# The softmax shift subtracted from adj^T square by square, into a second DRAM array

## Chip, cores and metric

One core of one Trainium2 chip runs the whole program. The metric is the device time of one execution in microseconds (us); the median of three runs of the kernel before is 11289.27 us (11283.2 to 11291.34).

## What is computed

Four graph layers over 3327 nodes with 128 features. All but the last 821 us of the execution go to the first, an attention layer with 128 heads (`d` below) of 8 elements each, whose scores are 3327 x 3327 in every head:

```python
q = (x @ Wq.T).reshape(d, n, h)
k = (x @ Wk.T).reshape(d, n, h)
v = (x @ Wv.T).reshape(d, n, h)
a = jnp.einsum('dnh,dmh->dnm', q, k) * scale
a = a + spatial_encoding + edge_encoding      # both are adj: a + 2 adj
a = jax.nn.softmax(a, axis=2)
out = jnp.einsum('dnm,dmh->dnh', a, v)
out = out.reshape(n, h * d)
return out @ Wo.T
```

The three later layers each multiply adj (or its transpose) with a 3327 x 128 array; layers 1, 2 and 3 read adj^T from DRAM, unshifted. The softmax needs a number per row n that is subtracted from the scores before the exponential. The kernel takes an upper bound: the largest adj in the row plus a bound of the row's products. It doesn't depend on the head, so it can be subtracted from adj itself.

## The kernel before

**Stages.** The first 451 us project x to q, k and v and write them to DRAM. The main stage (451 to 10332 us) is the attention. Then come the output projection (10332 to 10470 us) and the other layers, which stream adj^T and adj as "strips".

**Main stage.** The transposed scores are computed: partitions hold m, the free axis holds n. The columns n are cut into 7 blocks `c` of 476 (the last of 472). Within a block, 32 groups `g` of 4 heads follow each other, and within a group 13 pairs `q` of row tiles of 128 (26 tiles cover m). There are 7 x 32 x 13 = 2912 pairs. For each pair:

- VectorE *seeds* two PSUM banks with the adj^T tile minus the shift (`seed`, L640, tile `a` of 128 x 476, one for each of the 26 row tiles of the block);
- TensorE adds the products of the four heads one after the other (`scores`, L646), each time after ScalarE has taken the exponential of what is there (`exps`, L658 for two banks at once, L661 for one);
- TensorE multiplies the exponentials with the values (`values`, L699); VectorE copies the group's sums out (L707) and GpSimd's queue stores them (L711).

In the pairs q = 0, 4 and 8 one of the exponentials is made on VectorE instead (`hand_exp`): nine instructions L672, L674, L676, L678, four of L681, L683, spread over the pairs q, q+1, q+2 and q+3, in that order two, three, three and one.

**Order.** The stage is written out in program order by hand (`tc.manual_schedule`). Each engine and each queue works through its instructions in that order; nothing in the queues of SP (which issues most DMAs) and GpSimd is tied to the pair in which it is written, other than by what it waits for. `loads` issues the next group's keys, queries and values on SP (`load_qk`, 40 DMAs L553 to L557, and `load_v`, L570, in the pair q = 1), and GpSimd work on them (`negate_q` L565, `spread_v` L575, `all_here` L579) in the pair q = 4. The first scores of the next group wait for L579.

**Block ends.** In the last group of a block (g = 31) `load_shift` loads the next block's 476 shifts, broadcast to all partitions, and `load_adj` brings its 26 tiles `a` from `adjT` (L585), after each of which GpSimd subtracts the shift (L586). The pool of these tiles has 28 buffers: 26 in use, 2 ahead.

**Background squares.** adj^T is made during the main stage, one block ahead: 128 rows of adj at a time (a *square* `s`; 26 in all, the first four in the first stage, 22 in the main stage, planned at the block's first pair by `plan_squares`, one every 7 groups, in the groups 7k+1 and following). `plan(u, f)` runs f in program order at the pair u. A square takes four groups to load its rows (L285), transpose them on VectorE into `cols` (128 x 26 x 128, L290) and take row maxima (L294). Then `store` writes `cols` to `adjT` (L297, one DMA of 1664 KB), `gather` writes the maxima to DRAM (L301, 4 DMAs), `back` reads them back in another layout (`four`, L306, on SP), `finish` reduces `four` on VectorE (L310, L311) and stores the bound to `bound_d` (L312, on SP). Here store and gather stand at the last pair of the fourth group (u-1), back at pair 5 of the next one (u+5) and finish at its pair 12 (u+12). `cols` has one buffer.

**After the main stage.** `xs`, a second copy of x to which the layer's output is added (L892), is loaded into the pool `const` (L804), which is open from the start. The program puts that load where its memory is free: its three DMAs stand among the first on SP's queue. After the main stage, SP's queue has biases and weights (L811 to L853), two loads of attention output (`ot`, L877) with a strip of adj^T (L993) after each, then `w_raw` and `wo` (L861, L867), which TensorE's first transposes there need.

Of the kernel before, what the change touches and what calls it, by code (L numbers as in the profile page):

```python
# [10 lines left out]
F32 = mybir.dt.float32  # L11
# [6 lines left out]
ALU = mybir.AluOpType  # L18
# [4 lines left out]
P = 128  # L23
# [4 lines left out]
NT = 26  # L28
NP = NT * P
NQ = NT // 2  # L30
# [6 lines left out]
CW = 476  # L37
# [30 lines left out]
def rows_of(t):  # L68
    return P - 1 if t == NT - 1 else P
# [6 lines left out]
def pieces(m):  # L76

    return [(0, 112), (112, m)] if m == P - 1 else [(0, m)]


def width_of(c):

    return min(CW, N + 1 - c * CW)


def squares_of(c):

    return 0 if c < 0 else -(-min(CW * (c + 1), NP) // P)
# [3 lines left out]
def gnn_kernel(ctx: ExitStack, tc: tile.TileContext, x, adj, Wq, Wk, Wv, Wo, embed, layer,  # L92
               embed_bias, layer_bias, weight, bias, W_in, W_out, out):
    nc = tc.nc
    dram = ctx.enter_context(tc.tile_pool(name="dram", bufs=1, space=DRAM))
    const = ctx.enter_context(tc.tile_pool(name="const", bufs=1))
# [3 lines left out]

    adjT = dram.tile([NP, NP], F32, name="adjT")
    by_tile = adjT.rearrange("(p t) n -> t p n", t=NT)
    v_d = dram.tile([NP, HD], F32, name="v_d")
    n2_d = {s: dram.tile([GP], F32, name=f"n2{s}_d") for s in "qk"}
    kraw_d = dram.tile([H, GP], F32, name="kraw_d")
# [5 lines left out]
    bound_d = dram.tile([NP], F32, name="bound_d")  # L111
# [154 lines left out]
    class Square:  # L266
# [26 lines left out]
        def largest(self, j):  # L293
            nc.vector.tensor_reduce(self.rm[:, j:j + 1], self.rows, axis=AX.X, op=ALU.max)  # L294

        def store(self):
            nc.sync.dma_start(by_tile[:, :, self.s * P:(self.s + 1) * P].rearrange("t p n -> p t n"), self.cols)  # L297

        def gather(self):
            for i in range(4):  # L300
# [27 lines left out]
    with tc.tile_pool(name="a1", bufs=1) as a1, tc.tile_pool(name="a2", bufs=2) as a2, \  # L328
# [3 lines left out]
        xs = load_x(a1)  # L332
# [19 lines left out]
        for t0 in range(0, NT, 2):  # L352
            for s in "kq":
# [88 lines left out]
    with tc.tile_pool(name="d1", bufs=1) as d1, tc.tile_pool(name="d2", bufs=2) as d2, \  # L442
# [17 lines left out]
        with tc.If(loose > 0):  # L460
            for s in range(squares_of(0), NT):
                square(d2, s, d2)
            for t in range(NT):
                m = rows_of(t)
# [4 lines left out]
                with tc.For_i(0, HEADS, 1) as d:  # L469
# [3 lines left out]
                    for r in range(2):  # L473
                        for b in range(4):
# [9 lines left out]
                                                    op=ALU.max)  # L484
# [4 lines left out]
            for c in range(NC):  # L489
                c0 = c * CW  # L490
                w = min(CW, N - c0)
# [3 lines left out]
                with tc.For_i(0, HEADS, 1) as d:  # L495
# [12 lines left out]
                    for t in range(NT):  # L508
                        m = rows_of(t)
                        s = d_ps.tile([P, 4 * P], F32, name="ps_y")  # L510
# [13 lines left out]

    with tc.tile_pool(name="e1", bufs=1) as e1, tc.tile_pool(name="e_adj", bufs=28) as e_adj, \
            tc.tile_pool(name="e2", bufs=2) as e2, tc.tile_pool(name="e_e", bufs=1) as e_e, \
            tc.tile_pool(name="e_t", bufs=1) as e_t, tc.tile_pool(name="e_h", bufs=1) as e_h, \
            tc.tile_pool(name="e_ps", bufs=1, space=PSUM) as e_ps:  # L530
# [37 lines left out]
        def load_v(c, g):  # L568
            v = e2.tile([P, 4, NT * H], F32, name="VR", bufs=1)
            nc.sync.dma_start(v, bass.AP(tensor=v_d.tensor, offset=v_d.offset + 4 * g * N * H,  # L570
                                         ap=[[NT * H, P], [N * H, 4], [1, NT * H]]))
            return v

        def spread_v(c, g, v):
            nc.gpsimd.tensor_copy(VA[(c * NG + g) % 2][:, :, :, 0:H], v.rearrange("p j (t e) -> p t j e", e=H))  # L575

        def all_here(c, g):

            return nc.gpsimd.tensor_copy(seen, KT[(c * NG + g) % 2][:, :, 0].bitcast(F32))  # L579

        def load_adj(c, t, shift):

            a = e_adj.tile([P, CW], F32, name="a")
            w = width_of(c)
            nc.sync.dma_start(a[:, :w], by_tile[t, :, c * CW:c * CW + w])  # L585
            nc.gpsimd.tensor_tensor(a[:, :w], a[:, :w], shift[:, :w], op=ALU.subtract)  # L586
            return a

        def load_shift(c):
            s = e2.tile([P, CW], F32, name="shb", bufs=1)  # L590
            nc.sync.dma_start(s[:, :width_of(c)], bound_d[c * CW:c * CW + width_of(c)].unsqueeze(0)
                              .to_broadcast([P, width_of(c)]))
            return s

        with tc.If(loose < 1), tc.manual_schedule():
# [11 lines left out]
            n = len(pairs)  # L607
            adj_of, shift_of, v_of, e_of, here = {}, {}, {}, {}, {}
# [104 lines left out]
            def loads(u):  # L713

                c, g, q = pairs[u]
                k = c * NG + g
                if k + 1 < NC * NG:
                    nxt = divmod(k + 1, NG)
                    if q == 1:
                        load_qk(*nxt)  # L720
                        v_of[k + 1] = load_v(*nxt)
                    if q == 4:
                        negate_q(*nxt)
                        spread_v(*nxt, v_of.pop(k + 1))
                        here[k + 1] = all_here(*nxt)
                if c + 1 < NC and (g, q) == (0, 0):
                    plan_squares(c)
                if g == NG - 1 and c + 1 < NC:
                    if q == 0:
                        shift_of[c + 1] = load_shift(c + 1)  # L730
                        adj_of[c + 1] = []
                    while len(adj_of[c + 1]) < min(NT, 2 * q + 4):
                        adj_of[c + 1].append(load_adj(c + 1, len(adj_of[c + 1]), shift_of[c + 1]))


# [2 lines left out]
            def plan(u, f, *a):  # L738
                behind.setdefault(u, []).append((f, a))

            def plan_squares(c):
                for k, s in enumerate(range(squares_of(c), squares_of(c + 1))):
                    sq, u = Square(e_t, s), (c * NG + 7 * k + 1) * NQ
                    for j in range(4):
                        plan(u, sq.load, j)
                        plan(u + 7, sq.turn, j, 0)
                        plan(u + 11, sq.turn, j, 1)
                        plan(u + 12, sq.largest, j)
                        u += NQ
                    plan(u - 1, sq.store)  # L750
                    plan(u - 1, sq.gather)
                    plan(u + 5, sq.back)
                    plan(u + 12, sq.finish)

            v0 = load_v(0, 0)
            load_qk(0, 0)
# [12 lines left out]
            for i in range(-4, 4 * n + 15):  # L769
                u, j = in_slot(i)  # L770
# [16 lines left out]
                u = (i - 14) // 4  # L787
# [4 lines left out]
                if at % 2:  # L792
                    for k in (1, 2):
                        u, j = in_slot(i + k)
                        if 0 <= u < n:
                            scores(u, j)
                    u, r = ((i - 11) // 4, 0) if at == 3 else ((i - 13) // 4, 1)
# [3 lines left out]
                    loads(i // 4)  # L801


    xs = load_x(const)  # L804
    wts = ctx.enter_context(tc.tile_pool(name="wts", bufs=1))
    ones = wts.tile([P, 1], F32, name="ones")
    nc.vector.memset(ones, 1.0)

# [49 lines left out]
    with tc.tile_pool(name="f1", bufs=1) as f1, tc.tile_pool(name="f2", bufs=4) as f2, \  # L858
# [16 lines left out]
        for t0 in range(0, NT, 2):  # L875
# [5 lines left out]
                                    op=ALU.mult)  # L881
# [153 lines left out]
    with tc.tile_pool(name="g1", bufs=1) as g1:  # L1035
# [6 lines left out]
        a, aa = arr("a", D + 1), sm.new()  # L1042
# [12 lines left out]
        f = sm.div(sm.artanh(yn, L1_MAX_TANH), yn)  # L1055
# [33 lines left out]
    with tc.tile_pool(name="h1", bufs=1) as h1:  # L1089
# [4 lines left out]
        a, aa = arr("a", D + 1), sm.new()  # L1094
# [9 lines left out]
        f = sm.mul(sm.div(sm.artanh(pn, L2_MAX_TANH), pn), pf)  # L1104
# [8 lines left out]
        u, rr = arr("y"), sm.new()  # L1113
# [9 lines left out]
        t1 = sm.ts(sm.act(un, AF.Tanh), L2_MIN_NORM, ALU.max)  # L1123
# [10 lines left out]
    with tc.tile_pool(name="i1", bufs=1) as i1:  # L1134
# [67 lines left out]
```

## Time and profile before

| what | us |
|---|---|
| median of three runs | 11289.27 |
| the profiled execution | 11292.81 |
| its span, first to last instruction | 11290.9 |
| first stage | 451 |
| main stage, 451 to 10332 | 9881 |
| output projection, 10332 to 10470 | 138 |
| other layers | 821 |
| ScalarE busy in the main stage | 9810.12 |
| VectorE busy in the main stage | 7717.34 |
| GpSimd busy in the main stage | 1820.45 |

Times are those of one profiled execution, in microseconds unless marked ns. PE is TensorE, PEld its weight loads, DVE VectorE, ACT ScalarE, POOL GpSimd, SP the engine that issues most DMAs; SPq is the issue of a DMA. A group is listed by line, engine, operation and `out<-in` by the program's tile names. PEclk is the clock that TensorE was granted, as a share of full speed. In a timeline the columns are start, duration, engine, line, operation, and in square brackets the idle time before and what ended it.

### The profile page before, as it was taken

How to read it: one execution, taken by the hardware profiler on the slowest of the kernel's cores; microseconds unless marked ns; L12 is line 12 of the kernel's file. 1: busy time of each engine (PE TensorE's matmuls, PEld its weight loads, DVE VectorE, ACT ScalarE, POOL GpSimd, SP SyncE). 2: the span in 40 equal slices, each digit the busy share in tenths (PEclk: the TensorE clock that was granted, in tenths of full speed). 3: DMA queues.
4: the chain of work that ended last, by engine and by line, in shares of the span. 5: the costliest groups of instructions: out<-in, count | busy, mean ns of one | idle time of the engine just before them, and what ended most of it. 6: DMA issues, size and time to landing. Idle time of an engine off the chain costs nothing.

```text
span 11290.9 us, 205366 instructions
## 1 busy us (share of the span) xinstructions
PE 10774.9 (95%) x72980; PEld 3655.0 (32%) x72980; DVE 8367.4 (74%) x13563; ACT 10113.3 (90%) x13718; POOL 2021.8 (18%) x3261
## 2 busy tenths in 40 slices
PE   4599999999999999999999999999999999998779
PEld 2133333333333333333333333333333333334444
DVE  5577777778777787777777777777777777777633
ACT  3599999999999999999999999999999999996210
POOL 5211112111121111211112111121111211111000
PEclk8799999999999999999999999999999999999889
DMA  8755555555555554555555555555554544444447
GB/s 252 247 94 93 97 89 107 94 93 97 89 106 95 92 96 77 107 94 92 97 89 108 93 93 97 89 107 94 93 94 78 105 83 82 83 82 116 157 181 272
DMA packets 652681, 1243.36 MB, mean 110 GB/s; under 512 B 185966, under 2 KB 527990, under 8 KB 635148
## 3 DMA queue, kind: packets, MB, share of 16 engines
q1 hardware_dynamic: 609768, 1100.61, 50.0%
q0 software_dynamic: 41888, 129.51, 3.8%
q8 instruction: 591, 9.68, 0.4%
q14 instruction: 434, 3.56, 0.1%
HBM read 1082.90 MB, written 146.60 MB: 109 GB/s over the span
## 4 chain that ended last, share of the span: by engine, by line
ACT 72%; issue 12%; PE 9%; DVE 3%; DMA 1%; POOL 0%; SPq 0%; DVEq 0%; POOLq 0%; ACTq 0%
ACT e L658 60%; ACT e L661 11%; PE pu L995 5%; PE po L699 2%; PE S L646 1%; DVE e L681 1%; DVE S L640 0%; PE pu L947 0%; DMA ot<-oT_d 0%; DVE xs L982 0%; PE pu L970 0%; PE ps_y L891 0%; PE pu L958 0%; DVE h L676 0%; DMA QS<-qS_d 0%
## 5 line engine op out<-in xcount | busy, mean ns | idle before, releaser
L658 ACT ACTIVATE e<-S 128x952 f32<-128x952 f32 (+1 forms) x9408 | 8757.9, 1180 | 54.5 <-PE S L646 53.6
L699 PE MATMUL po<-e,VA 128*9 128x476 f32 (+1 forms) x46592 | 5750.7, 566 | 19.0 <-DVE OS L707 2.6
L640 DVE COPY S<-a 128x476 f32<-128x476 f32 (+1 forms) x5824 | 3817.0, 655 | 1975.8 <-ACT e L658 1503.3
L646 PE MATMUL S<-QS,KT 64*128 64x476 f32 (+1 forms) x23296 | 4858.2, 450 | 70.0 <-DVE S L640 60.7
L646 PEld LDWEIGHTS S<-QS,KT 64*128 64x128 f32 x23296 | 2431.8, 184 | 5198.2 <-issue 1640.3
L661 ACT ACTIVATE e<-S 128x476 f32<-128x476 f32 (+1 forms) x3808 | 2424.2, 788 | 10.8 <-PE S L646 10.7
L681 DVE SCALAR_TENSOR_TENSOR e<-e,h 128x476 f32<-128x476 f32 (+1 forms) x2016 | 1411.1, 700 | 46.1
L711 POOL DMA_DIRECT2D oT_d<-OS x896 | 471.2, 531 | 4505.8 <-DVE OS L707 4460.2
L699 PEld LDWEIGHTS po<-e,VA 128*9 128x9 f32 x46592 | 691.0, 88 | 1577.8 <-issue 1485.6
L565 POOL TENSOR_SCALAR QS<-QS 32x476 fp32r<-32x476 f32 (+1 forms) x1344 | 850.5, 633 | 1513.0 <-DMA QS<-qS_d 868.4
L672 DVE TENSOR_SCALAR h<-S 128x476 f32<-128x476 f32 (+1 forms) x672 | 439.1, 653 | 78.7 <-PE S L646 6.5
L681 DVE SCALAR_TENSOR_TENSOR e<-h 128x476 f32<-128x476 f32 (+1 forms) x672 | 455.1, 677 | 0.0
L676 DVE TENSOR_TENSOR h<-h,h 128x476 f32<-128x476 f32 (+1 forms) x672 | 446.4, 664 | 0.0
L683 DVE SCALAR_TENSOR_TENSOR e<-e,h 128x476 f32<-128x476 f32 (+1 forms) x672 | 442.3, 658 | 0.0
L131 ACT COPY uT<-pu 128x494 f32<-128x494 f32 (+1 forms) x12 | 6.6, 547 | 427.2 <-PE pu L995 427.2
L575 POOL COPY VA<-VR 128x832 f32<-128x832 f32 x224 | 206.5, 922 | 920.6 <-DMA VR<-v_d 650.4
L995 PE MATMUL pu<-strip,h 128*128 128x494 f32 (+2 forms) x728 | 293.9, 564 | 38.9 <-ACT h L928 38.9
L674 DVE TENSOR_SCALAR h<-h 128x476 f32<-128x476 f32 (+1 forms) x672 | 307.9, 458 | 23.2
L995 PE MATMUL pu<-strip,y 128*128 128x494 f32 (+2 forms) x728 | 295.4, 568 | 29.1 <-DVE y L982 18.0
L678 DVE TENSOR_SCALAR h<-h 128x476 int32<-128x476 f32 (+1 forms) x672 | 294.0, 438 | 22.9
L586 POOL TENSOR_TENSOR a<-a,shb 128x476 f32<-128x476 f32 (+1 forms) x182 | 242.1, 1362 | 252.7 <-DMA a<-adjT 202.3
L290 DVE STREAM_TRANSPOSE cols<-rows 128x416 f32<-128x416 f32 x208 | 203.6, 984 | 21.3 <-DMA rows<-in_adj_dram 14.0
(185 smaller groups left out, 2404.9 us busy)
## 6 DMA issues: line engine op xcount, KB each, us to landing
KT<-kS_d SPq DMA_DIRECT2D x1792, 208.0 KB
KT<-kS_d SPq DMA_DIRECT2D x1792, 104.0 KB
VR<-v_d SPq DMA_DIRECT2D x224, 416.0 KB
strip<-adjT POOLq DMA_DIRECT2D x39, 1663.5 KB, 7.0
strip<-adjT SPq DMA_DIRECT2D x36, 1663.5 KB
QS<-qS_d SPq DMA_DIRECT2D x3072, 14.9 KB
QS<-qS_d SPq DMA_DIRECT2D x1536, 29.8 KB
adjT<-cols SPq DMA_DIRECT2D x26, 1664.0 KB
```

The source lines that it names most:

```text
L565: nc.gpsimd.tensor_scalar(QS[b][r0:r0 + 32, j + 1, :w], QS[b][r0:r0 + 32, j, :w].bitcast(F32), -1.0, 0.0, op0=ALU.mult, op1=ALU.add)
L640: touch(u, [r], nc.vector.tensor_copy(bank(u, r), adj_of[c][2 * q + r][:, :w]))
L646: x = nc.tensor.matmul(bank(u, r), KT[b][64 * r:64 * r + 64, max(0, j - 1), q * P:(q + 1) * P], QS[b][64 * r:64 * r + 64, j, :w], start=Fa ...
L658: touch(u, (0, 1), nc.scalar.activation(e[:, :, :w], S[:, odd:even + 1, :w], AF.Exp, scale=2.0))
L661: touch(u, [r], nc.scalar.activation(e[:, 1 - r, :w], bank(u, r), AF.Exp, scale=2.0))
L672: touch(u, [1], nc.vector.tensor_scalar(f, bank(u, 1), LOG2_E2, EXP_LEAST, op0=ALU.mult, op1=ALU.max))
L676: nc.vector.tensor_tensor(f, f, whole, op=ALU.subtract)
L681: nc.vector.scalar_tensor_tensor(e, f if k == 4 else e, EXP_C[k], f, op0=ALU.add, op1=ALU.mult)
L683: nc.vector.scalar_tensor_tensor(e, e, EXP_C[0], power.bitcast(F32), op0=ALU.add, op1=ALU.mult)
L699: nc.tensor.matmul(po[32 * j:32 * j + H + 1, :w], VA[k % 2][:, 2 * pairs[v][2] + of, j, :], e_of[v, j][:, 1 - of, :w], start=(q == 0 and r ...
L711: nc.gpsimd.dma_start(oT_d[:, d * N + c * CW:d * N + c * CW + w], o[32 * j:32 * j + H + 1, :w])
L995: nc.tensor.matmul(pu[c][:, :w], y[:m, t, :], s[:m, c * AW:c * AW + w], start=(t == 0), stop=(t == NT - 1))
```

## The change

The shift is subtracted from a square while it lies in `cols`, and the result goes to a second DRAM array `adjS`; the blocks then load from `adjS`. The first four squares (columns 0 to 511) are made in the first stage and are not in `adjS`. So block 0 loads and subtracts as before, block 1 subtracts in its first 36 columns only and loads the other 440 from `adjS` by a DMA of their own, and blocks 2 to 6 subtract nothing.

```diff
+    adjS = dram.tile([NP, NP], F32, name="adjS")
+    shifted_by_tile = adjS.rearrange("(p t) n -> t p n", t=NT)
...
-        def store(self):
-            nc.sync.dma_start(by_tile[:, :, self.s * P:(self.s + 1) * P].rearrange("t p n -> p t n"), self.cols)
+        def store(self, to=by_tile):
+            nc.sync.dma_start(to[:, :, self.s * P:(self.s + 1) * P].rearrange("t p n -> p t n"), self.cols)
+
+        def spread(self):
+            self.on_all = self.small.tile([P, P], F32, name="on_all")
+            nc.sync.dma_start(self.on_all, bound_d[self.s * P:(self.s + 1) * P].unsqueeze(0).to_broadcast([P, P]))
+
+        def shift(self, t0, t1):
+            nc.gpsimd.tensor_tensor(self.cols[:, t0:t1, :], self.cols[:, t0:t1, :],
+                                    self.on_all.unsqueeze(1).to_broadcast([P, t1 - t0, P]), op=ALU.subtract)
...
-    with tc.tile_pool(name="e1", bufs=1) as e1, tc.tile_pool(name="e_adj", bufs=28) as e_adj, \
+    with tc.tile_pool(name="e1", bufs=1) as e1, tc.tile_pool(name="e_adj", bufs=30) as e_adj, \
...
+        def unshifted(c):
+
+            return max(0, min(width_of(c), squares_of(0) * P - c * CW))
+
         def load_adj(c, t, shift):
 
             a = e_adj.tile([P, CW], F32, name="a")
-            w = width_of(c)
-            nc.sync.dma_start(a[:, :w], by_tile[t, :, c * CW:c * CW + w])
-            nc.gpsimd.tensor_tensor(a[:, :w], a[:, :w], shift[:, :w], op=ALU.subtract)
+            w, m, c0 = width_of(c), unshifted(c), c * CW
+            if m:
+                nc.sync.dma_start(a[:, :m], by_tile[t, :, c0:c0 + m])
+                nc.gpsimd.tensor_tensor(a[:, :m], a[:, :m], shift[:, :m], op=ALU.subtract)
+            if m < w:
+                nc.sync.dma_start(a[:, m:w], shifted_by_tile[t, :, c0 + m:c0 + w])
             return a
...
-                    while len(adj_of[c + 1]) < min(NT, 2 * q + 4):
+                    while len(adj_of[c + 1]) < min(NT, 2 * q + 6):
...
-                    plan(u - 1, sq.store)
-                    plan(u - 1, sq.gather)
-                    plan(u + 5, sq.back)
-                    plan(u + 12, sq.finish)
+                    for k, f in ((0, sq.store), (0, sq.gather), (3, sq.back), (7, sq.finish), (10, sq.spread)):
+                        plan(u + k, f)
+                    for k in range(NQ):
+                        plan(u + NQ + k, sq.shift, 2 * k, 2 * k + 2)
+                    plan(u + 2 * NQ + 1, sq.store, shifted_by_tile)
...
-    xs = load_x(const)
     wts = ctx.enter_context(tc.tile_pool(name="wts", bufs=1))
+    xs = load_x(wts)
```

`load_shift` returns nothing where a block has no unshifted columns, and loads only those otherwise. The pool of the tiles `a` grows from 28 to 30 buffers, in the room that `xs` held. `shift` covers 2 of the 26 tiles of `cols`, so a square has 13 of them, planned at the pairs 0 to 12 of the group after the one with `finish`. In the queues as built, GpSimd has three of the 13 ahead of that group's L711, two between L711 and its L565, and eight after its L579. SP has `four` (back) directly behind the group's `load_qk` and `load_v`, as before, then the bound's store, then `spread`. On VectorE, `finish` stands between the seeds of the pairs 7 and 8, after L683, instead of at pair 12. After the main stage the load of `xs` comes first on SP's queue, then the biases, weights and the two `ot`, then `w_raw` and `wo`, and the strips behind these.

More of the change, by code (lines that the diff above doesn't have):

```diff
@@ L579, in all_here @@
             return nc.gpsimd.tensor_copy(seen, KT[(c * NG + g) % 2][:, :, 0].bitcast(F32))
+        def unshifted(c):
+            return max(0, min(width_of(c), squares_of(0) * P - c * CW))
         def load_adj(c, t, shift):
             a = e_adj.tile([P, CW], F32, name="a")
-            w = width_of(c)
-            nc.sync.dma_start(a[:, :w], by_tile[t, :, c * CW:c * CW + w])
-            nc.gpsimd.tensor_tensor(a[:, :w], a[:, :w], shift[:, :w], op=ALU.subtract)
+            w, m, c0 = width_of(c), unshifted(c), c * CW
[4 more added lines that the diff above has]
+                nc.sync.dma_start(a[:, m:w], shifted_by_tile[t, :, c0 + m:c0 + w])
             return a
         def load_shift(c):
+            m = unshifted(c)
+            if m == 0:
+                return None
             s = e2.tile([P, CW], F32, name="shb", bufs=1)
-            nc.sync.dma_start(s[:, :width_of(c)], bound_d[c * CW:c * CW + width_of(c)].unsqueeze(0)
-                              .to_broadcast([P, width_of(c)]))
+            nc.sync.dma_start(s[:, :m], bound_d[c * CW:c * CW + m].unsqueeze(0).to_broadcast([P, m]))
             return s
```

## The prediction

> **What bounds the kernel now.** I read the page's busy shares and its chain of waits first.
>
> ```profile
> PE 10774.9 (95%) x72980; PEld 3655.0 (32%) x72980; DVE 8367.4 (74%) x13563; ACT 10113.3 (90%) x13718; POOL 2021.8 (18%) x3261
> ```
>
> The chain gives ScalarE 72% of the span. The table of windows says where it isn't busy: a block end (last and first group), a group pair inside a block, and a group with a square's store and reduction (block 2, group 5).
>
> ```profile
> 1818.00:1912.00 94.00, 87.48 (x609) 26.12 (x601) 76.36 (x106) 85.92 (x116) 47.86 (x49) 0.96 0.64 143
> 3228.00:3322.00 94.00, 87.42 (x590) 25.72 (x588) 73.58 (x102) 83.28 (x114) 46.21 (x49) 0.93 0.62 143
> ...
> 2480.00:2574.00 94.00, 93.74 (x672) 29.61 (x670) 72.63 (x117) 94.00 (x128) 14.12 (x25) 1.00 0.46 81
> ...
> 3508.20:3552.30 44.10, 43.86 (x317) 13.89 (x320) 33.47 (x58) 44.10 (x61) 7.32 (x12) 1.00 0.67 96
> ```
>
> After the length come PE, PEld, DVE, ACT, POOL, PEclk. Inside a block ScalarE is busy 94.00 of 94.00, so it sets the end and a stall of it can't be made up. At the six block ends it is busy 85.92, 83.28, 85.84, 86.92, 85.03 and 86.51: idle 50.5 us in all. Those are the places where POOL works 46 to 48 us instead of 14. VectorE's timeline, first from a block end and then from inside a block, shows how:
>
> ```profile
> 1854.32 1.29 DVE L678 TENSOR_SCALAR h<-h 128x476 int32<-128x476 f32 x1
> ...
> 1858.41 4.59 DVE L681 SCALAR_TENSOR_TENSOR e<-e,h 128x476 f32<-128x476 f32 x3
> ...
> 3538.95 0.41 DVE L678 TENSOR_SCALAR h<-h 128x476 int32<-128x476 f32 x1
> ...
> 3528.20 2.02 DVE L681 SCALAR_TENSOR_TENSOR e<-e,h 128x476 f32<-128x476 f32 x3
> ```
>
> While POOL runs L586 the instructions of the hand-made exponentials take two to three times as long; two seeds L640 stay at 1.4. So the subtraction costs through VectorE, not by being late.
>
> **Removed: the subtraction at block ends.** 26 L586 at six ends are 156; 50.5 / 156 = 0.324 us of ScalarE each (median 1.242 us of POOL). Block 1 keeps 36 of 476 columns: 26 x 0.324 x 36/476 = 0.6. **Gain -50**; by the starts of the groups' first activations the six ends exceed the usual 43.8 a group by 57, so bounds -40 to -57. Two more buffers for `a` add nothing: no seed waits long for a tile there, and without POOL a tile is ready sooner. The 26 extra narrow DMAs of block 1 run when SP has only tiles to load.
>
> **Added: 13 shifts for each of 22 squares, 286.** No 128x256 subtraction is in the trace; by L586, 1.242 x 256/476 = 0.67 us, 8.7 us of POOL a square. They are not spread over 13 pairs: nothing ties POOL to the pairs, so they run in bursts of three, two and eight, the eight after L579, some 31 to 37 us into a group, over the hand-made exponentials of the pairs 9 to 11. By the ratio above, 0.324 x 256/476 x 286 = **+50**, as much as is gained. Below: 0, if VectorE's idle quarter takes them (the six L565 in every group cost ScalarE nothing visible). Above: from 1851 to 1867 us six L586 cost ScalarE idle times of 1.50, 2.23 and 0.81, 0.76 each: 0.76 x 256/476 x 286 = 117. I take the mean row, being over both kinds of pair.
>
> [...] Were every shift to block VectorE for its whole time unhidden, the estimate would be 22 x 8.7 = 191 in place of 50.
>
> **Moved: finish, from pair 12 to pair 7.** This decides. Here are SP, VectorE and POOL in block 2, group 5, whose first activation starts at 3508.19:
>
> ```profile
> 3538.53 0.39 SPq L570 DMA_DIRECT2D VR<-v_d  x1
> 3538.97 0.71 SPq L306 DMA_DIRECT2D four<-rowmax_d  x1
> ...
> 3531.69 0.65 DVE L683 SCALAR_TENSOR_TENSOR e<-e,h 128x476 f32<-128x476 f32 x1
> 3533.45 1.42 DVE L640 COPY S<-a 128x476 f32<-128x476 f32 x2 [1.12 <-ACT e L661]
> ...
> 3548.60 0.15 DVE L310 TENSOR_REDUCE b<-four 128x1 f32<-128x4 f32 x1
> ...
> 3542.03 1.05 POOL L575 COPY VA<-VR 128x832 f32<-128x832 f32 x1 [4.24 <-DMA VR<-v_d]
> ```
>
> `four` is loaded behind the group's 40 key and query DMAs and VR, so SP reaches it 30.8 us into the group. Planning `back` at pair 3 instead of 5 doesn't alter that: both stand behind `load_qk` at pair 1. VR, issued just before, has landed when POOL starts at 3542.03; `four` lands about 3542.2. Today L310 comes at 3548.60, 6 us later, and waits for nothing. Changed, it stands right after L683 of pair 7, at 3532.34. VectorE works in order, so it stands still until 3542.2, and the seeds of pair 8 behind it. L310 and L311 take 0.34: these seeds start at 3542.6 instead of 3533.45. TensorE, in order too, stops at pair 8's second bank, and ScalarE runs dry after the activation of 3535.17, about 3535.6. A seed (0.65), pair 8's second product and the two behind it (three of 0.45) and gaps of 0.2 bring the next activation to 3544.8: **9.2 us lost**. Bounds 8.2 (landing half a microsecond before POOL's start, some slack) to 10.2.
>
> After such a pause TensorE gets a lower clock:
>
> ```profile
> 8350.00:8360.00 10.00, 8.41 (x50) 2.36 (x50) 6.08 (x10) 7.44 (x10) 1.00 (x2) 0.83 0.98 223
> ```
>
> 0.17 of 10 us is 1.7 us of clock lost after a stall of 2.6; TensorE, busy 9809 of 9881 us in this stage, has nothing to spare. I add **1.7**; bounds 0 and 6.6 (0.07 of 94 us at the worst block end). Per square 10.9, times 22: **+240** (bounds 180 to 370).
>
> [...]
>
> **The other DMAs and queues.** Store and gather move one pair, but SP has nothing between: same order, same time. Behind the bound's store SP now holds `spread`, waiting for that store; behind it are the next group's loads at its pair 1, and the bound goes out 6 us earlier than today (L312 at 3548.97), which covers it. The new store of 1664 KB waits for the 13th shift, about 38 us into its group, and is over before or shortly after the next keys are asked for. Its like, L297, today delays a group's L579 to 35 us, and the row above still has ScalarE at 44.10 of 44.10: zero; the cover is about 8 us there and more here. On POOL five shifts (3.3 us) stand before L565 of their group, which mostly waits for data; L579 then ends near 31 us.
>
> **xs.** Its load leaves the first stage, where the page's first slice moves 252 GB/s: 1651 KB, 6.6 us if all on the path; I take **-3**, bounds -6.6 to 0. It comes first after the main stage, but there w_raw and wo overtake two strips:
>
> ```profile
> 10338.80 19.11 SPq L993 DMA_DIRECT2D strip<-adjT  x1
> 10364.73 0.33 SPq L861 DMA_DIRECT2D w_raw<-in_L_gnn_weight_dram  x1
> ...
> 10369.10 0.45 PE L863 MATMUL ps_t<-ident,w_raw 128*128 128x128 f32 x1 [37.33 <-DMA wo<-in_L_gnn_Wo_dram]
> ```
>
> Ahead of wo on SP stand 3327 KB of strips less and 1651 more: 1676 KB less at half of the 373 GB/s of 10335 to 10368 us is **-9**; bounds -19 (the strip's issue) to +8 (xs alone on the path).
>
> **Sum.** 11290.9 - 50 + 50 + 240 - 3 - 9 = 11518.9. The medians of the runs lie 1.6 under the span: **11517 us**, 2.0% slower.
>
> **The rivals.**
> [...] The shifts cost 117 and the clock 5 us a square more than taken: 11517 + 67 + 73 = about 11650 (5 being near the bound of 6.6, less what falls into the pause; 22 x 3.3 = 73). For it: the burst of eight meets three hand-made pairs. Against: six L565 in a row cost nothing today. Chance 0.11.
> *The stall is partly covered.* ScalarE loses only half of 10.9, for instance because `four` lands sooner in a quieter queue: 11517 - 120 = 11397. The queue is the same as today's, which speaks against. 0.09.
> *The other side: finish doesn't wait.* Place: SP's queue between L553 and L306. If `four` had landed by 3533.45, 25 us into the group, the 240 are gone: 11277, and 11227 where the shifts hide too. It decides from about 2 us a square, where 22 x 2 eats the gain of 50. Against it, L306 is issued 5.5 us after that point. 0.06.
> *The change doesn't do what it says.* Block ends keep their idle time because seeds wait for tiles from adjS: 11567. There the tiles' DMAs are today's. 0.04.
>
> **How the numbers follow.** The forecast gets 0.70. The range 11420 to 11620 holds it but for 0.04, the last rival, and some 0.1 of the first two: 0.8 in all. A measurement of this kernel can tell 0.2% (23 us) from no change. Faster by more: 0.04, most of the other side; within: 0.02; slower: 0.94.
>
> **What would show it.** Right: L310 with about 10 us of idle before it, ended by `four`, 22 times; ScalarE idle 9 us in each such group, with PEclk below 1.00; block ends with ScalarE near 94 of 94; L861 issued before 10364.73 plus the main stage's growth. Wrong: L310 without idle time, or groups with eight shifts in a row that lose more than 4 us.

## The result, and the profile after

The changed kernel takes 11476.75 us (median of four runs, 11474.29 to 11481.12) where the kernel before took 11286.24 us beside it. The ratio is 1.0169 with a 95% interval of 1.0151 to 1.0187: 1.7% slower. The forecast was 11517 us, with a range of 11420 to 11620. The profiled execution ran 11474.29 us, its span is 11472.2, so 181.3 more than the span of before.

The page's busy shares first:

```profile
PE 10797.5 (94%) x72980; PEld 3664.2 (32%) x72980; DVE 8332.8 (73%) x13563; ACT 10115.1 (88%) x13718; POOL 2045.1 (18%) x3417
```

ScalarE has as much work as before (10113.3) in a longer span: what was added is waiting. The list of waits, of the kernel before and then of the changed one (us in total, times, longest), says for what:

```profile
ACT e L658 <- PE S L646: 53.6, 43, 2.8
```

```profile
POOL cols L307 <- DMA on_all<-bound_d: 259.8, 22, 12.9
DVE b L321 <- DMA four<-rowmax_d: 208.4, 22, 10.7
ACT e L678 <- PE S L666: 203.1, 63, 9.6
```

In the list of before VectorE never waits at L310, which is now L321, and ScalarE (L658 is now L678) waits for TensorE for 53.6 us in 43 pieces. Now VectorE stands still 22 times, once a square, 9.5 us on average, and ScalarE 203 us. With the activations of one bank (10.7 us before L661, now 37.4 before L681) ScalarE's waits for TensorE grow from 64 to 240 us. GpSimd's own wait for the tile `on_all`, a square's shifts as `spread` loads them, is new too and costs nothing, as the run finish12 shows.

The timeline of the changed kernel in block 2, group 5, whose first activation starts at 3570.6, shows one of the 22. The rows come from the queue of SP, VectorE and ScalarE:

```profile
3600.72 0.39 SPq L581 DMA_DIRECT2D VR<-v_d  x1
3601.16 0.51 SPq L317 DMA_DIRECT2D four<-rowmax_d  x1
...
3594.15 0.65 DVE L703 SCALAR_TENSOR_TENSOR e<-e,h 128x476 f32<-128x476 f32 x1
3604.22 0.16 DVE L321 TENSOR_REDUCE b<-four 128x1 f32<-128x4 f32 x1 [9.42 <-DMA four<-rowmax_d]
...
3604.96 1.40 DVE L660 COPY S<-a 128x476 f32<-128x476 f32 x2
...
3597.61 0.88 ACT L681 ACTIVATE e<-S 128x476 f32<-128x476 f32 x1
3606.91 0.96 ACT L678 ACTIVATE e<-S 128x952 f32<-128x952 f32 x1 [8.43 <-PE S L666]
```

The load of `four` is issued 30.6 us into the group, behind VR. The reduction that waits for it stands in front of the seeds of pair 8, so these come 34.4 us into the group, and ScalarE has nothing from 3598.5 to 3606.9.

The table of windows of the changed kernel: the group with the stall, the group with the shifts, two block ends, and the stretch around the stall in pieces of 3 us.

```profile
3570.60:3624.60 54.00, 45.48 (x317) 14.65 (x320) 33.91 (x57) 44.21 (x61) 9.43 (x15) 0.91 0.50 81
3624.60:3669.40 44.80, 43.93 (x316) 13.90 (x316) 35.28 (x55) 44.10 (x60) 15.75 (x22) 1.00 0.61 118
...
1860.00:1954.00 94.00, 93.79 (x673) 29.22 (x672) 69.00 (x115) 94.00 (x129) 20.98 (x47) 1.00 0.70 144
3304.00:3398.00 94.00, 93.86 (x674) 30.04 (x672) 69.42 (x115) 94.00 (x128) 14.02 (x25) 1.00 0.63 144
...
3600.00:3603.00 3.00, 0.00 (x0) 0.00 (x0) 0.00 (x0) 0.00 (x0) 0.08 (x1) 0.50 0.55 136
3603.00:3606.00 3.00, 0.34 (x2) 0.34 (x3) 1.65 (x4) 0.00 (x0) 1.01 (x2) 0.50 0.30 63
3606.00:3609.00 3.00, 3.00 (x13) 0.78 (x13) 2.41 (x5) 0.96 (x1) 0.00 (x0) 0.50 0.01 0
3609.00:3612.00 3.00, 3.00 (x26) 0.74 (x24) 1.85 (x4) 2.75 (x4) 0.00 (x0) 0.99 0.03 5
```

The group with the stall is 54.0 us long, its ScalarE busy 44.2; the one with the shifts 44.8, where 43.8 is usual; the block ends, where ScalarE was idle 7 to 11 us before, are full. And TensorE's granted clock (third column from the right) is 0.50 during the pause and, in this stall, for some 3.4 us after it.

Where the 181.3 us come from, by the starts of the groups' first activations (a stage's sum over the groups, after minus before):

| place | predicted | measured |
|---|---|---|
| six block ends | -50 | -57 |
| 22 groups with the wait for `four` | +240 | +228 |
| 22 groups with shifts, and those behind them | +50 | +6.5 |
| start of the main stage | -3 | -0.9 |
| from its end to the program's end | -9 | +3.4 |
| all the rest | 0 | +1 |
| sum | +228 | +181 |

### The profile page after: what moved, and what is told of

Read it like the earlier page. It is cut to its first block, busy times and chain, and to the rows that moved or that the text cites. A ratio compares the mean times of both kernels' runs of the same rounds, so it can differ in the third digit from the quotient of the medians.

```text
span 11472.2 us, 205583 instructions
## 1 busy us (share of the span) xinstructions
PE 10797.5 (94%) x72980; PEld 3664.2 (32%) x72980; DVE 8332.8 (73%) x13563; ACT 10115.1 (88%) x13718; POOL 2045.1 (18%) x3417
## 4 chain that ended last, share of the span: by engine, by line
ACT 45%; PE 35%; issue 7%; DMA 5%; DVE 3%; SPq 1%; POOL 0%; POOLq 0%; DVEq 0%; ACTq 0%
ACT e L678 38%; PE po L719 16%; PE S L666 13%; ACT e L681 7%; PE pu L1016 5%; DMA QS<-qS_d 2%; DMA KT<-kS_d 1%; DVE S L660 1%; DMA four<-rowmax_d 1%; DVE e L701 0%; SPq L564 0%; PE pu L968 0%; DMA rowmax_d<-rm 0%; DVE OS L727 0%; DMA ot<-oT_d 0%
## 5 line engine op out<-in xcount | busy, mean ns | idle before, releaser
L678 ACT ACTIVATE e<-S 128x952 f32<-128x952 f32 (+1 forms) x9408 | 8749.2, 1176 | 204.2 <-PE S L666 203.1
L660 DVE COPY S<-a 128x476 f32<-128x476 f32 (+1 forms) x5824 | 3815.4, 655 | 1980.3 <-ACT e L678 1508.8
L681 ACT ACTIVATE e<-S 128x476 f32<-128x476 f32 (+1 forms) x3808 | 2421.2, 785 | 37.6 <-PE S L666 37.4
L701 DVE SCALAR_TENSOR_TENSOR e<-e,h 128x476 f32<-128x476 f32 (+1 forms) x2016 | 1375.1, 682 | 46.1
L576 POOL TENSOR_SCALAR QS<-QS 32x476 fp32r<-32x476 f32 (+1 forms) x1344 | 851.8, 634 | 1446.2 <-DMA QS<-qS_d 775.4
L703 DVE SCALAR_TENSOR_TENSOR e<-e,h 128x476 f32<-128x476 f32 (+1 forms) x672 | 439.8, 654 | 0.0
L694 DVE TENSOR_SCALAR h<-h 128x476 f32<-128x476 f32 (+1 forms) x672 | 313.1, 466 | 23.2
L698 DVE TENSOR_SCALAR h<-h 128x476 int32<-128x476 f32 (+1 forms) x672 | 286.7, 427 | 22.9
L307 POOL TENSOR_TENSOR cols<-cols,on_all 128x256 f32<-128x256 f32 x286 | 236.4, 859 | 260.0 <-DMA on_all<-bound_d 259.8
```

Of the source, the lines that this page charges most:

```text
L576: nc.gpsimd.tensor_scalar(QS[b][r0:r0 + 32, j + 1, :w], QS[b][r0:r0 + 32, j, :w].bitcast(F32), -1.0, 0.0, op0=ALU.mult, op1=ALU.add)
L660: touch(u, [r], nc.vector.tensor_copy(bank(u, r), adj_of[c][2 * q + r][:, :w]))
L678: touch(u, (0, 1), nc.scalar.activation(e[:, :, :w], S[:, odd:even + 1, :w], AF.Exp, scale=2.0))
L681: touch(u, [r], nc.scalar.activation(e[:, 1 - r, :w], bank(u, r), AF.Exp, scale=2.0))
L701: nc.vector.scalar_tensor_tensor(e, f if k == 4 else e, EXP_C[k], f, op0=ALU.add, op1=ALU.mult)
L703: nc.vector.scalar_tensor_tensor(e, e, EXP_C[0], power.bitcast(F32), op0=ALU.add, op1=ALU.mult)
```

## The experiments

All run on the chip beside the kernel before. "Main" is the time from the first activation of the main stage to the end of the last one, in the profiled run, "rest" from there to the program's end.

| run | median us | ratio to before, 95% | main | rest |
|---|---|---|---|---|
| before | | | 9874.1 | 961.7 |
| the change | 11476.75 | 1.0169 (1.0151 to 1.0187) | 10052.8 | 965.1 |
| finish12 | 11239.08 | 0.9952 (0.9938 to 0.9965) | 9820.1 | 963.2 |
| before_finish7 | 11551.96 | 1.0224 (1.0208 to 1.0239) | 10136.5 | 961.9 |
| finish9 | 11345.75 | 1.0045 (1.0030 to 1.0061) | 9927.1 | 965.2 |
| back_first | 11259.20 | 0.9971 (0.9960 to 0.9982) | 9840.8 | 962.1 |
| no_shift | 11242.69 | 0.9957 (0.9943 to 0.9971) | 9819.4 | 961.8 |
| shift_twice | 11265.51 | 0.9973 (0.9963 to 0.9982) | 9841.7 | 967.4 |
| shift_by4 | 11241.17 | 0.9955 (0.9942 to 0.9969) | 9819.9 | 962.2 |
| xs_early | 11240.99 | 0.9954 (0.9940 to 0.9968) | 9819.5 | 962.8 |
| back_first_no_shift | 11243.11 | 0.9955 (0.9941 to 0.9969) | 9820.1 | 969.7 |
| shift_four | 11593.42 | 1.0265 (1.0251 to 1.0279) | 10169.9 | 964.8 |
| back_first_by4 | 11274.05 | 0.9987 (0.9978 to 0.9996) | 9858.5 | 963.1 |
| back_first_by1 | 11234.73 | 0.9955 (0.9942 to 0.9969) | 9818.7 | 966.5 |

### Is it the place of `finish`?

**finish12**: the changed kernel with `finish` back at pair 12.

```diff
-  for k, f in ((0, sq.store), (0, sq.gather), (3, sq.back), (7, sq.finish), (10, sq.spread)):
+  for k, f in ((0, sq.store), (0, sq.gather), (3, sq.back), (12, sq.finish), (12, sq.spread)):
```

> The changed kernel with finish and spread at pair 12 in place of 7 and 10; all else is kept. Theory A (VectorE stands still at finish until four lands, 10.5 us a square, 232 us in all): the reduction of finish has no idle time before it, no group with a reduction is longer than 44.3 us, the block ends stay without idle time of ScalarE, and the time is the one before, 11286, less 57 (block ends), plus about 9 (shifts) and 3 (tail): 11240 us, 0.4% faster than before. Rival B (the background's second store and the shifts cost, wherever finish stands): it stays near 11476.

It took 11239.08. VectorE no longer waits at L321, and GpSimd waits longer for `on_all` than in the changed kernel:

```profile
POOL cols L307 <- DMA on_all<-bound_d: 391.6, 22, 20.8
```

No group is over 44.3 us but the first and two that are long in every run (block 5, groups 18 and 19). The main stage is 232.7 us shorter than the changed kernel's: 10.6 a square. The rest of the change is a gain: this kernel is 0.5% faster than the one before, and GpSimd's wait of 18 us a square lies on no path.

**before_finish7**: the kernel before, with the planned places of the change and nothing else of it.

```diff
-  plan(u - 1, sq.store)
-  plan(u - 1, sq.gather)
-  plan(u + 5, sq.back)
-  plan(u + 12, sq.finish)
+  plan(u, sq.store)
+  plan(u, sq.gather)
+  plan(u + 3, sq.back)
+  plan(u + 7, sq.finish)
```

> The kernel before with store and gather at pair 0, back at pair 3 and finish at pair 7; nothing of the second array. Theory A: the stall comes without the rest of the change, 22 x 10.5 = 232 us more: 11518 us, with some 9.5 us of idle time before each of the 22 reductions. Rival B: 11286.

11551.96, 34 more than expected; its list of waits:

```profile
DVE b L310 <- DMA four<-rowmax_d: 232.9, 22, 12.2
```

The move alone costs 262.4 us of main stage, 11.9 a square, in a kernel without second array and shifts. The wait is 10.6 us a square here instead of 9.5, as `four` is reached a microsecond later in the group, and the loss is larger by as much.

**finish9**: the changed kernel with `finish` two pairs later, which takes 6.8 us (two pairs of 3.4) out of the wait.

```diff
-  for k, f in ((0, sq.store), (0, sq.gather), (3, sq.back), (7, sq.finish), (10, sq.spread)):
+  for k, f in ((0, sq.store), (0, sq.gather), (3, sq.back), (9, sq.finish), (10, sq.spread)):
```

> The changed kernel with finish at pair 9. VectorE gets there some 30.4 us into the group, four lands at about 33.6. Theory A: a wait of 3 us a square, of which 3 to 4 us are lost with the clock: 11240 + 22 x 3.5 = 11317 us (11300 to 11330). If the loss came from something that a wait only starts (the clock alone, a broken rhythm of the hand-made exponentials), it would be nearly as large as at pair 7, 11450; if waits of a few us are absorbed, 11240.

11345.75, 16 over the range. Its list of waits:

```profile
DVE b L321 <- DMA four<-rowmax_d: 68.9, 22, 4.4
```

So three points stand side by side: a wait of 3.1, 9.5 and 10.6 us a square costs 4.9, 10.6 and 11.9 us (against the same kernel with `finish` at pair 12). The loss is the wait and 1.1 to 1.7 us more, nearly independent of its length: of that surplus the expectation had allowed 1 us at most.

**back_first**: `finish` stays at pair 7, but `back` is planned ahead of the group's loads, so that `four` is there in time.

```diff
-  for k, f in ((0, sq.store), (0, sq.gather), (3, sq.back), (7, sq.finish), (10, sq.spread)):
+  for k, f in ((0, sq.store), (0, sq.gather), (0, sq.back), (7, sq.finish), (10, sq.spread)):
```

> The changed kernel with back directly behind gather, at pair 0, ahead of the group's key and query loads on SP; finish stays at pair 7. Theory A: four lands some 10 us into the group, well before pair 7, so the reduction doesn't wait: 11240 us, though SP now waits 2 to 3 us for gather to land before it issues the group's loads. Rival C (pair 7 is a bad place on VectorE whatever four does): 11476. Rival B: 11476.

```profile
3504.62 0.38 SPq L317 DMA_DIRECT2D four<-rowmax_d  x1
```

`four` is issued 8.3 us into the group (of block 2, group 5, here) and the wait of L321 is gone, with `finish` where the change has it. So it is not the place as such, but the place against the queue of SP. But 11259.20 is 20 us more than with `finish` at pair 12, and the trace puts them into the groups with the shifts, about 1 us each on average. That led to the next question.

### What does a shift cost?

**no_shift**, **shift_twice** and **shift_by4** change the shifts of finish12: none, each made twice, and the same work in 7 instructions of 512 columns instead of 13 of 256.

```diff
-  for k in range(NQ):
-      plan(u + NQ + k, sq.shift, 2 * k, 2 * k + 2)
```

```diff
   for k in range(NQ):
       plan(u + NQ + k, sq.shift, 2 * k, 2 * k + 2)
+      plan(u + NQ + k, sq.shift, 2 * k, 2 * k + 2)
```

```diff
-  for k in range(NQ):
-      plan(u + NQ + k, sq.shift, 2 * k, 2 * k + 2)
+  for k in range(0, NQ, 2):
+      plan(u + NQ + k, sq.shift, 2 * k, min(2 * k + 4, NT))
```

> This is the run with finish and spread at pair 12 (11239 us) without the 286 shifts: the columns 512 to 3326 of the scores go into the exponential without the bound subtracted; the copies to adjS, spread and everything else stay. Theory D (the shifts lengthen VectorE's instructions by some 37 us in the whole run, but mostly inside VectorE's idle time of 0.7 us a pair): the groups with shifts exceed the others by 0.3 to 1.0 us, about 9 us in all, so 11230. Theory P, the prediction's term (0.324 us of ScalarE for 1.24 us of GpSimd, +50 in all): 11189. Which end it is near to measures the price of the 286 shifts.

> Finish and spread at pair 12, and each shift made twice (the bound is subtracted two times from the columns 512 to 3326): 572 shifts, in bursts of about 16. Theory D: VectorE's slack is used up by the first shift in the worst pairs, so the second 286 cost more than the first 286 did (9 us), 10 to 40 in all: 11249 to 11279. Theory P (each shift costs ScalarE the same 0.17 us): 11289, and as much below in the run without shifts. If a shift costs nothing at all: 11239.

> Finish and spread at pair 12, and the same work in 7 shifts of 4 tiles (128x512) instead of 13 of 2 tiles, so each holds VectorE up for about 1.4 us in place of 0.7. Theory D (what counts is the work that meets VectorE, against its idle time): 11236 to 11249. Rival L (the length of one shift decides, since the block-end subtractions that cost 0.37 us each were as long): 7 x 22 = 154 shifts at 0.37 make 57, in place of 9, so about 11287.

Measured were 11242.69, 11265.51 and 11241.17; in the main stage, where the scatter of the first stage and of the tail is left out, the 286 shifts of finish12 cost 0.7 us, 572 cost 22.3, and 154 long ones 0.5. Theory P is out: at 0.17 us a shift it asked for 50. Theory D has the direction, and its range in two of the three; for the run without shifts it expected 11230, a price of 9 us, and there is none to be seen. How far the shifts lengthen VectorE's work can be counted in the traces, over its instructions that overlap a shift: in finish12 28 of them grow, by 7 us in all, in shift_twice 172, by 69. (The page's busy time of VectorE says less: 8297.6 without shifts, 8316.2 in finish12, but 8323.5 in xs_early below, which has the same shifts.) So 7 us vanish in VectorE's idle time, and of the next 62 a third comes through. Rival L, which asked for 57 in the run with long shifts, is out as it was put: there 39 instructions grow by 21 us, and these vanish as well. In finish12 `on_all` lands late, and the burst of eight lies 36 to 42 us into its group, over the pairs 11 and 12.

**back_first_no_shift**: the shifts are taken out of back_first, by the first of the three edits above; there the burst lies at 29 to 37 us, over the pairs 9 to 11.

> The run with back at pair 0 and finish at pair 7 (11259 us), without the 286 shifts: the bound is not subtracted from the columns 512 to 3326. There the burst of eight shifts lay some 29 to 37 us into its group, over the pairs 9 to 11, and those 22 groups lost 1.2 us each, 27 in all; with finish at pair 12 the burst lay at 36 to 42 us and the groups lost nothing. Theory place (the same shifts cost 1.2 us a square where they meet the hand-made exponentials of the pairs 9 to 11): those groups lose nothing here, 11236 to 11242. Rival: the earlier back and finish cost it, not the shifts: 11257 to 11261.

11243.11, a microsecond past the expected range, but its main stage is 9820.1: the groups with shifts lose nothing, and all 20.7 us that back_first has more are the shifts'. The rival, that an earlier `back` and `finish` cost them, is out. The same 286 instructions cost 0.7 us in one place and 20.7 in another. The count says why: in back_first 138 of VectorE's instructions grow, by 60 us in all, in finish12 28. All 138 belong to the hand-made exponentials, which are nearly through in the pairs 11 and 12; of the seeds (L660), some 160 of which overlap a shift in either run, none grows.

**shift_four**: each shift of finish12 made four times.

```diff
   for k in range(NQ):
-      plan(u + NQ + k, sq.shift, 2 * k, 2 * k + 2)
+      for _ in range(4):
+          plan(u + NQ + k, sq.shift, 2 * k, 2 * k + 2)
```

> Finish and spread at pair 12, and each shift made four times (the bound is subtracted four times from the columns 512 to 3326): 52 x 0.8 = 42 us of GpSimd a square, spread over two groups, about as much as the 26 subtractions of a block end (32 us) with their loads. So far 286 shifts cost 1 us in the main stage and the second 286 cost 22. Theory D (what counts is how much of VectorE's idle time is left): the third and fourth 286 cost about the block end's price, 0.29 us of ScalarE for 1 us of GpSimd, 22 x 21 x 0.29 = 134 on top of 11265, less where they fall into easy pairs: 11330 to 11420. Rival K (a shift of this form is cheap whatever its number, and the block ends' loss has another cause than the subtraction's time): the line goes on with 22 a dose, 11265 + 44 = 11309.

11593.42, far above both. Its list of waits names what neither theory had in view:

```profile
PE S L666 <- POOL seen L590: 262.6, 23, 14.3
```

Its table of windows shows the two groups of one square:

```profile
3662.40:3706.50 44.10, 43.69 (x314) 13.81 (x312) 35.49 (x55) 43.86 (x60) 30.39 (x41) 1.00 0.50 83
3706.50:3764.10 57.60, 44.15 (x313) 13.79 (x312) 36.58 (x55) 44.69 (x60) 26.29 (x37) 0.92 0.54 104
```

The second group's L576 and L590, for which the scores of the next group wait, stand in GpSimd's queue behind 32 shifts (28 us), and this group is 13.8 us over the usual 43.8. Of the 15.9 us that a square costs in the main stage, 14.8 are lost so: as a price of the collisions the run says nothing. But its first group is a find. GpSimd is busy 30.4 of 44.1 us, and the group loses 0.3 us (1.1 on average over the 22). This is a block end of the kernel before, in the same view:

```profile
3233.60:3284.20 50.60, 47.74 (x318) 14.00 (x320) 39.24 (x55) 44.57 (x60) 23.20 (x26) 0.90 0.74 185
```

With less GpSimd work, 23.2 us, it loses 6.8, and VectorE is busy 39.2 instead of 35.5. So neither GpSimd's time nor its share sets the price; the instructions differ in length, 1.24 us there and 0.74 here.

**back_first_by4** and **back_first_by1** test that where the shifts do cost something: the subtraction of back_first in 7 instructions of 512 columns, and in 26 of 128.

```diff
-  for k in range(NQ):
-      plan(u + NQ + k, sq.shift, 2 * k, 2 * k + 2)
+  for k in range(0, NQ, 2):
+      plan(u + NQ + k, sq.shift, 2 * k, min(2 * k + 4, NT))
```

```diff
-  for k in range(NQ):
-      plan(u + NQ + k, sq.shift, 2 * k, 2 * k + 2)
+  for k in range(NT):
+      plan(u + NQ + k // 2, sq.shift, k, k + 1)
```

> Back at pair 0, finish at pair 7, and the same subtraction in 7 shifts of 4 tiles (128x512, some 1.3 us each) instead of 13 of 2 tiles (0.74 us). In the run with 2 tiles the last eight lay over the hand-made exponentials of the pairs 9 to 11, and a square cost 1.2 us (main stage 9837 us against 9816 without shifts). Theory L (an instruction of VectorE that meets a GpSimd one waits for its end, so the length of the single GpSimd instruction sets how much each of the 24 is lengthened: by 0.4 us for a shift of 2 tiles, by 0.5 to 0.9 for the 1.24 us subtraction of the block ends): 2 to 3.5 us a square, main stage 9860 to 9890, time 11282 to 11315. Rival W (the GpSimd time that meets VectorE decides, however it is cut): 20 to 27 us as before, 11255 to 11262.

> The same with 26 shifts of one tile (128x128; from 0.74 us for 256 and 1.29 us for 512 columns, 0.46 us each by a straight line, so 12 us of GpSimd a square instead of 9.6). Theory L: each instruction of VectorE that meets one is lengthened by 0.2 us, so a square costs 0 to 0.7 us, 11239 to 11254. Rival W: 12/9.6 of 20 to 27 us, 11264 to 11274.

The page's groups for the shifts of back_first, by4 and by1 give GpSimd's busy time, the mean and the wait:

```profile
L307 POOL TENSOR_TENSOR cols<-cols,on_all 128x256 f32<-128x256 f32 x286 | 257.4, 931 | 180.1 <-DMA on_all<-bound_d 179.9
```

```profile
L307 POOL TENSOR_TENSOR cols<-cols,on_all 128x512 f32<-128x512 f32 (+1 forms) x154 | 202.1, 1336 | 166.5 <-DMA on_all<-bound_d 166.3
```

```profile
L307 POOL TENSOR_TENSOR cols<-cols,on_all 128x128 f32<-128x128 f32 x572 | 308.7, 575 | 163.8 <-DMA on_all<-bound_d 163.6
```

GpSimd works longest in by1 and shortest in by4. The main stage goes the other way: 9818.7 in by1, 9840.8 in back_first, 9858.5 in by4, against 9820.1 without shifts. VectorE's timeline in block 2, group 6 shows the same three instructions of a hand-made exponential under the burst, in back_first, by4 and by1:

```profile
3569.94 0.66 DVE L696 TENSOR_TENSOR h<-h,h 128x476 f32<-128x476 f32 x1
3570.63 0.82 DVE L698 TENSOR_SCALAR h<-h 128x476 int32<-128x476 f32 x1
3571.37 1.18 DVE L701 SCALAR_TENSOR_TENSOR e<-h 128x476 f32<-128x476 f32 x1
```

```profile
3575.03 1.24 DVE L696 TENSOR_TENSOR h<-h,h 128x476 f32<-128x476 f32 x1
3576.30 1.38 DVE L698 TENSOR_SCALAR h<-h 128x476 int32<-128x476 f32 x1
3577.59 1.73 DVE L701 SCALAR_TENSOR_TENSOR e<-h 128x476 f32<-128x476 f32 x1
```

```profile
3561.87 0.65 DVE L696 TENSOR_TENSOR h<-h,h 128x476 f32<-128x476 f32 x1
3562.55 0.71 DVE L698 TENSOR_SCALAR h<-h 128x476 int32<-128x476 f32 x1
3563.17 0.91 DVE L701 SCALAR_TENSOR_TENSOR e<-h 128x476 f32<-128x476 f32 x1
```

Undisturbed they take 0.64, 0.41 and 0.65. L698 grows by 0.30, 0.41 and 0.97 us under instructions of 0.46, 0.74 and 1.29 (medians of L307 in by1, finish12 and by4; in back_first itself GpSimd's are lengthened too, to a median of 0.90). No instruction of VectorE grows by more than 0.33, 0.58 and 1.13 us in the three runs (by1, back_first, by4), less than one instruction of GpSimd, though in back_first eight stand in a row (7.80 us). Rival W, by which the time of GpSimd counts however it is cut, is out in both runs: it asked for more in by1, which costs nothing, and for the same in by4, which costs 38 us of main stage instead of 21. Theory L has the direction in both. Its size for by4 was too high (11282 to 11315 expected, 11274.05 measured): the four long instructions of that burst meet fewer of VectorE's than eight short ones. By the count 187 instructions grow in by1, by 35 us in all, 138 in back_first, by 60, and 88 in by4, by 69. So theory D isn't out either: in these three runs the main stage grows with the sum of these, once it is more than some 35 us, and short instructions make the sum smaller because each meeting is shorter.

### Does the late load of xs matter?

**xs_early**: finish12 with xs in the pool that is open from the start, and 28 buffers for `a`.

```diff
-  tc.tile_pool(name="e_adj", bufs=30) as e_adj
+  tc.tile_pool(name="e_adj", bufs=28) as e_adj
...
-  while len(adj_of[c + 1]) < min(NT, 2 * q + 6):
+  while len(adj_of[c + 1]) < min(NT, 2 * q + 4):
...
+    xs = load_x(const)
     wts = ctx.enter_context(tc.tile_pool(name="wts", bufs=1))
-    xs = load_x(wts)
```

> Finish and spread at pair 12, and xs back in the pool that is open from the start, with 28 buffers for a in place of 30 and two tiles less ahead. The prediction had xs's late load gain 9 us in the output projection and 3 in the first stage; the trace of the changed kernel shows the end of the program 3.4 us later after the main stage than before, and the main stage's start 0.9 us earlier. By the prediction's terms this run loses 12: 11251. By the trace it gains 3.4 - 0.9: 11236 to 11237. The 28 buffers are expected to cost nothing at the block ends.

11240.99 beside 11239.08 for finish12: no difference, and not the 11251 of the prediction's terms. Over all runs the rest after the main stage takes 961.7, 961.9 and 962.8 with the early load and 961.8 to 969.7, mean 964.6, with the late one. A gain of 9 is excluded; a loss of some 2 is likely and smaller than the scatter of the late ones.

## Why the prediction was right, and where it was not

**What bounds the kernel**: right. In the main stage the stalls of ScalarE came out as time: its waits for TensorE grew by 176 us, the stage by 178.7.

**The wait for `four`, +240**: right, and shown by moving it. The chain was as written down: L317 behind VR 30.6 us into the group (30.8 was read from before), the seeds of pair 8 at 34.4 (34.4 worked out), ScalarE back at 36.3 (36.6). For the 9.2 us lost the trace has 8.43 and, one activation later, 1.37. It measured 228, or 10.4 a square against 10.9 (10.6 against finish12). Taking `finish` out of the wait removes it (finish12, back_first), and putting the wait into the old kernel makes it (before_finish7).

**The clock, 1.7 a square within that**: right in kind, and too small on average. In the rows above TensorE starts at 3605.7 at 0.50 and has full clock from about 3609, and half the work of 3.4 us is 1.7. No other of the 22 stalls had it back as soon: over all of them the trace's clock comes back 3.4 to 5.9 us after TensorE starts again, 4.5 on average, which is 2.2 us of work, and up to 6.6 in before_finish7. There TensorE is busy through a whole stretch of 4 us and still has 0.50:

```profile
3641.00:3645.00 4.00, 4.00 (x22) 0.95 (x16) 2.84 (x6) 2.13 (x3) 0.00 (x0) 0.50 0.06 6
```

The surplus of 1.1 to 1.7 us over the wait in all three runs with a stall is of this size and somewhat below it; that it is the clock alone is argued, not shown, since seeds that ran ahead take some of the loss away.

**The block ends, -50**: right in kind, 7 too small. ScalarE's idle time in the windows was taken, and the starts of the groups, which give 57 and stood as the bound, were what came out.

**The shifts, +50**: this step failed, and the size of this term was 43 of the 47 us by which the sum was too high. (The wait and the block ends were another 19 too high; the start and the tail erred the other way by 14.5 and hid most of that, which was luck.) The prediction carried 0.324 us of ScalarE for a 1.242 us subtraction over to the shifts in proportion to their columns: "By the ratio above, 0.324 x 256/476 x 286 = +50". The price is not proportional to GpSimd's time. It is 57 us for 156 long instructions at block ends, 0.7 for 286 short ones over the pairs 11 and 12, 20.7 for the same ones over the pairs 9 to 11, and nothing for 572 shorter ones there. The lower bound, "0, if VectorE's idle quarter takes them", was the one to take. In the changed kernel itself the burst lies at 27 to 33 us (medians), 92 instructions of VectorE grow by 37 us in all, and 6.5 us remained. The estimate of 191, by the sum of GpSimd's time, was further off still: in these runs the price went by the number of instructions met, the length of each one and the idle time that takes up the first of it.

**Tail -9 and start -3**: wrong in sign or not to be seen. `w_raw` and `wo` were indeed issued earlier, and the first transposes after the main stage started 33.8 us after its last copy of sums (L727) instead of 36.6. The 2.8 us were not kept: the degree reductions of the strips on VectorE (L1019, 3.58 us each) now stand among the last projections, and the first products of the next layer began 132.2 us after that copy instead of 129.7. That these reductions are the cause is read from the order in the trace and was not tried. The start of the main stage moved by -0.9 and lies between 451.8 and 460.3 over all runs, so a term of -3 can't be seen.

**The rivals**: shifts and a clock that cost more than taken, a stall of which only half is lost and block ends that keep their idle time are out by the table. The rival of the other side needed `four` to land by 25 us into the group; back_first is that case, made on purpose, and takes 11259.20, between the 11277 and 11227 that were worked out for it.

**What is left of the change**: with `finish` at pair 12 it gains 0.5%. Six of the versions above, two of them without the shifts, lie between 11234.73 and 11243.11 and can't be told apart. The groups 18 and 19 of block 5, 3 to 6 us long over the usual in every run, before included, were not looked into.

## What to carry to other kernels

Before a small instruction is moved forward in an engine that works in order, look at when its operand was *issued* on the queue that loads it, not at where the load is written: a 0.16 us reduction, five pairs early, cost 10.4 us each time, because its load stood behind 41 others. In this kernel, background work on GpSimd beside a busy VectorE was cheapest cut into short instructions (main stage 9818.7 us with 128 columns each, 9858.5 with 512), or put where VectorE ran few instructions that collide (0.7 us for the 286 shifts in one place, 20.7 in another); its price went by what it met and how long each one was, not by its sum. And a price taken from one place of the trace holds for that place: carry it over with its conditions, or bound it by a row that has them.

## What the hardware showed that was not expected

Cutting GpSimd's work finer made it longer (308.7 us of L307 in place of 202.1) and the kernel faster (main stage 9818.7 in place of 9858.5). A VectorE instruction that met a shift was lengthened by at most about the length of one (0.33, 0.58 and 1.13 us under shifts of 0.46, 0.74 and 1.29), though eight stood in a row in back_first, and there GpSimd's own were lengthened too, from a median of 0.74 to 0.90. Seeds were not lengthened: in the changed kernel 173 of them overlap a shift, and none takes more than 0.002 us over the usual 0.656.

What came on top of a wait was nearly the same for a short one and a long one (1.7, 1.1 and 1.3 us for 3.1, 9.5 and 10.6, in finish9, the change and before_finish7), so a short wait was dear for its length. Nor did the lower clock come with long pauses alone: in finish9, where TensorE stood still for 1.9 to 4.3 us, the granted clock fell to 0.50 in 21 of the 22 pauses, the shortest of them 2.0 us, and its mean over the run was 0.973 (0.977 in finish12).
